# Order of a list-scheduled graph kernel: hand-written ranks or a table of ranks

## Chip, core and metric

One core of a Trainium2 chip runs the whole kernel. The metric is the device time in microseconds (us): the median of three executions, 4420.69 us for the kernel before (4419.77 to 4421.27). The profile is one more execution of the same program; its span, from the first to the last instruction, is 4417.6 us.

## What is computed

Sixteen graphs (B = 16) of 1024 nodes with 256 features pass through four layers. In front of each layer stands a normalisation over the features and a ReLU, and each layer's result is added to x. All graphs share one adjacency matrix.

```python
# layers 0, 1 (one head) and 3 (four heads of 64): graph attention
h = x @ W
e = leaky_relu(e_src[:, :, None] + e_dst[:, None, :])
attention = softmax(where(adj, e, -big), axis=-1)
out = relu(attention @ h)          # layer 0;  elu in layers 1 and 3
# layer 2: eight heads of 32, masked dot-product attention, then
x = layernorm(x + t); h = relu(x @ w1 + b1); x = layernorm(x + h @ w2 + b2)
# around every layer
h = maximum(layernorm(x), 0.0);  x = x + layer(h)
```

## The kernel before

The kernel is written as *operations*. An operation is a small bundle of instructions of one engine with a guessed duration (`cost`), the operations it comes after, the buffers it takes and gives back, and a `rank`. When all are laid, `play()` walks them through a model of the five engines (PE, DVE, ACT, POOL and SP, the queue that issues transfers) and sends out the instructions in the order in which the model began them. Every engine of the chip then runs its instructions in that order and waits at semaphores. All this happens on the host while the program is built. What it decides is the order alone.

```python
DELAY = (0.2, 0.12, 0.14, 0.06, 2.0)
SWITCH = {None: 0.2, 132: 0.21, 32: 0.125}   # PE: change of the form of matmuls
SLACK = 0.1
STAY = 4.0
PLAYS = 8

def choose(open_ops, time, begin, key, slack):
    best = None
    for eng in range(5):
        could = [...]                        # (earliest start, op) of what can begin
        if could:
            last = min(c[0] for c in could) + slack
            at, o = min((c for c in could if c[0] <= last), key=lambda c: key(c[1]))
            ...
def forward(rank):
    ...
    at, o = choose(open_ops, time, begin,
                   lambda o: rank[o.number] + STAY * (o.eng == PE and o.form != form), SLACK)
    ...
def play():
    rank, best = [o.rank for o in ops], None
    for _ in range(PLAYS):
        result = forward(rank)
        if best is None or result[0] < best[0]:
            best = result
        rank = backward(*result)             # latest starts become the next ranks
    ...                                      # then o.fn() in the order of the best play
```

PE's operations have three forms: full (128 x 128 array, `form=None`), 132 (layer 2's scores, 32 rows) and 32 (products with 32 columns). The stages of the graphs are interleaved; between the beginning and the end the order repeats with a period of one graph:

```python
for b in range(1, B - 3):
    order += [(2, b), (1, b + 1), (3, b), (0, b + 2)]     # (layer, graph)
```

A tile of 128 rows that leaves a layer enters the next one at once. This is the end of layer 1 and the way into layer 2, with the durations that the model takes; `TH` = 4 tiles make one half `n` of a graph:

```python
# gat_out, layer 1
inv = op(DVE, 0.08, ...)                     # 1 / sum
o   = op(ACT, 0.73, ...)                     # exp and relu of the product
add = op(DVE, 0.98, ...)                     # two additions into x
way_in(s.next, t, rank, [add])
# way_in, layer 2, for each tile
m_op (DVE 0.54) -> r_op (POOL 1.15) -> norm (ACT 0.4)
# when the four tiles of the half are there
transpose_rows(...)                          # PE 0.88 (tp), ACT 0.92 (hT)
two_values(s, n, ...)                        # PE 3.48, then ACT 0.92
queries_keys(s, m, n, ...)                   # m = 0, 1: PE 3.43 each, then ACT 0.92
```

A stage of layer 3 begins with its sources: `tpr` turns them on PE, DVE copies them, a transfer stores them (`kept`) and two transfers spread them over the partitions (`r`). DVE then makes the weights `p` from `r`, and PE multiplies them (`acc` L1091, `sums` L1115).

Of the kernel before, what the change touches and what calls it, by code (L numbers as in the profile page):

```python
# [28 lines left out]
U8 = mybir.dt.uint8  # L29
I32 = mybir.dt.int32  # L30
AF = mybir.ActivationFunctionType
ALU = mybir.AluOpType
AX = mybir.AxisListType
PSUM = bass.MemoryType.PSUM

P = 128
# [3 lines left out]
H2 = 8  # L40

GAT_HIGH, GAT_LOW = 2.0**45, 2.0**-45
INV_HIGH, INV_LOW = 2.0**80, 2.0**-90


def rows(w):
# [239 lines left out]
def fast_path(tc, bad, x, adj, l0_w, l0_a, l1_w, l1_a, w_qkv, ln1_g, ln1_b, ln2_g, ln2_b, w1, b1, w2, b2, l3_w, l3_a, out):  # L286

    nc = tc.nc
    B, N, C = x.shape
    assert B > 6  # L290
    NT, KC, HALF = N // P, C // P, 512
    NH, TH = N // HALF, HALF // P
    D2 = C // H2
    SCALE2 = 1.0 / float(D2) ** 0.5
    H3, _, HS3 = l3_w.shape
# [4 lines left out]
    with ctx:  # L300
# [9 lines left out]
        xs = {}  # L310
# [99 lines left out]
        WX = {0: wx0, 1: wx1, 2: qkv_sb[:, :, 2 * C :], 3: wx3}  # L410
# [15 lines left out]

        ops = []
        PE, DVE, ACT, POOL, SP = range(5)  # L430

# [5 lines left out]

        BEFORE_END = 0.1

        SLACK = 0.1  # L440

        STAY = 4.0
        PLAYS = 8

        class Op:
# [35 lines left out]
# [4 lines that stand above are left out]
                could = []  # L485
                for o in open_ops[eng]:
                    at = begin(o)
                    if at is not None:
                        could.append((max(at, time[eng]), o))
                if could:  # L490
                    last = min(c[0] for c in could) + slack
                    at, o = min((c for c in could if c[0] <= last), key=lambda c: key(c[1]))
                    if best is None or at < best[0]:
                        best = (at, o)
            assert best, "nothing can begin"
            open_ops[best[1].eng].remove(best[1])
            return best

        def forward(rank):

            time, form, held = [0.0] * 5, 0, {DVE: 0.0, POOL: 0.0}
            ready = [0.0] * len(ops)
            missing = [len(o.after) for o in ops]
            taken = {
                ring: [[h for h in ring.first if h.place == i] for i in range(ring.bufs)] if ring.is_set else [list(ring.first)]
                for ring in R.values()
            }
            left, free = {}, {}
            for ring in R.values():
                for h in ring.first:  # L510
                    left[h], free[h] = len(h.enders), 0.0
            open_ops = [[o for o in ops if o.eng == eng and not o.after] for eng in range(5)]
            played = []

            def places_of(ring):

                times = []
                for i, holds in enumerate(taken[ring]):
                    if not holds or not left[holds[-1]]:
                        times.append((free[holds[-1]] if holds else 0.0, i))  # L520
                return sorted(times)

            def begin(o):
                at = ready[o.number]
                if o.eng == POOL or o.tiles:
                    at = max(at, held[POOL + DVE - o.eng])
                for i, h in enumerate(o.takes):
                    ring = h.ring
                    again = sum(g.ring is ring for g in o.takes[:i])
                    if ring.is_set:  # L530
                        times = places_of(ring)
                        if again >= len(times):
                            return None
                        at = max(at, times[again][0])
                        continue
                    k = len(taken[ring][0]) + again
                    if ring.ordered and h.number != k:
                        return None
                    if k >= ring.bufs:
                        old = taken[ring][0][k - ring.bufs]  # L540
                        if left[old]:
                            return None
                        at = max(at, free[old])
                return at

            for _ in ops:
                at, o = choose(open_ops, time, begin, lambda o: rank[o.number] + STAY * (o.eng == PE and o.form != form), SLACK)
                cost = o.cost
                if o.eng == PE and o.form != form:
                    cost, form = cost + SWITCH[o.form], o.form  # L550
                if o.tiles:
                    held[o.eng] = at + cost - BEFORE_END
                time[o.eng] = at + cost
                played.append((at, cost, o))
                end = at + cost + o.delay
                for h in o.takes:
                    place = places_of(h.ring)[0][1] if h.ring.is_set else 0
                    taken[h.ring][place].append(h)
                    left[h], free[h] = len(h.enders), 0.0
                for h in o.ends:  # L560
                    left[h] -= 1
                    free[h] = max(free[h], end)
                for u in o.users:
                    missing[u.number] -= 1
                    ready[u.number] = max(ready[u.number], end if u.eng != o.eng else end - ITSELF)
                    if not missing[u.number]:
                        open_ops[u.eng].append(u)
            return max(time), played, taken

        def backward(total, played, taken):  # L570

            before = [list(o.after) for o in ops]
            for ring, places in taken.items():
                for holds in places:
                    for old, h in zip(holds, holds[1 if ring.is_set else ring.bufs :]):
                        before[h.taker.number] += [o for o in old.enders if o is not h.taker]
            waiting = [0] * len(ops)
            for list_of in before:
                for o in list_of:
                    waiting[o.number] += 1  # L580
            length, key = [0.0] * len(ops), [0.0] * len(ops)
            for at, cost, o in played:
                length[o.number], key[o.number] = cost, -(at + cost)
            time, ready, latest = [0.0] * 5, [0.0] * len(ops), [0.0] * len(ops)
            open_ops = [[o for o in ops if o.eng == eng and not waiting[o.number]] for eng in range(5)]
            for _ in ops:
                at, o = choose(open_ops, time, lambda o: ready[o.number], lambda o: key[o.number], 0.0)
                time[o.eng] = at + length[o.number]
                latest[o.number] = total - time[o.eng]
                for a in before[o.number]:  # L590
                    waiting[a.number] -= 1
                    ready[a.number] = max(ready[a.number], time[o.eng] + a.delay)
                    if not waiting[a.number]:
                        open_ops[a.eng].append(a)
            return latest

        def play():
            rank, best = [o.rank for o in ops], None
            for _ in range(PLAYS):
                result = forward(rank)  # L600
                if best is None or result[0] < best[0]:
                    best = result
                rank = backward(*result)
            for ring, places in best[2].items():
                for i, holds in enumerate(places):
                    for h in holds:
                        h.place = i
            for _, _, o in best[1]:
                for h in o.takes:
                    h.t = h.make(h.place) if h.ring.is_set else h.make()  # L610
                o.fn()
            return best
# [27 lines left out]
        class Stage:  # L640
# [33 lines left out]
            @property  # L674
            def v(self):
                used = NT * self.heads * (self.hs + 1)
                return self.vh.t[:, :used].rearrange("p (t h d) -> p t h d", t=NT, h=self.heads)

            @property
            def e(self):  # L680
                return self.eh.t

            @property
            def y(self):
                return self.yh.t
# [727 lines left out]
        E = B - 1  # L1413
# [100 lines left out]
        at = 0.0  # L1514
        for k, s in enumerate(stages):
            begin = at
# [11 lines left out]
            if k + 1 < len(stages) and stages[k + 1].layer == 0:  # L1528

                nxt = stages[k + 1]  # L1530
                for t in range(NT):
                    here = x_in[nxt.b]
                    way_in(nxt, t, begin + 1.0 + 3.0 * t, [here[t * len(here) // NT]] + (s.mains[t * len(s.mains) // 12 :][:1] or stages[k - 1].mains[-1:]))
        play()


# [55 lines left out]
```

## Time and profile before

| | |
|---|---|
| median time | 4420.69 us |
| span of the profile | 4417.6 us |
| PE busy | 4314.3 us |
| DVE busy | 3376.2 us |
| ACT busy | 2002.7 us |
| POOL busy | 1274.0 us |
| matmul instructions | 28105 |

The page gives busy time and instructions of each engine, and the chain of work that ended last with shares by engine and by line. The timeline gives instructions in order of time: start, duration of the merged group, engine, line, tiles written and read, count, and in brackets the idle time of the engine before it with what ended it. The end of a matmul is modelled; the distance from one start to the next is the safer length. PEclk is the clock granted to TensorE, 1.00 being full.

### The profile page before, as it was taken

The page shows a single profiled execution, that of the slowest core. Times are in us where ns is not written, and L with a number is a line of the kernel's source. Part 1 is how long each engine was busy: PE and PEld are TensorE (multiplying, and loading weights), DVE is VectorE, ACT ScalarE, POOL GpSimd, SP SyncE. Part 2 cuts the span into 40 slices and gives each one's busy share as a digit, 9 for nine tenths or more (in the row PEclk, how much of TensorE's full clock was granted, in tenths as well). Part 3 has the DMA queues.
Part 4 walks back from the last instruction along what each step waited for, and adds up shares of the span by engine and source line. Part 5 has one row for each costly group of instructions (what it writes and reads, how often), then busy time and mean ns, then how long its engine had stood idle before and what let it go on. Part 6 is the DMA issues. An engine that isn't in the chain of part 4 may idle for free.

```text
span 4417.6 us, 70358 instructions
## 1 busy us (share of the span) xinstructions
PE 4314.3 (98%) x28105; PEld 2232.0 (51%) x28105; DVE 3376.2 (76%) x5834; ACT 2002.7 (45%) x3091; POOL 1274.0 (29%) x2025
## 2 busy tenths in 40 slices
PE   9999999999999999999999999999999999999998
PEld 7735364553545535455354554545545455464433
DVE  7577977778777787777877778777787777858798
ACT  4452635435354353543535435353453534545351
POOL 3222231422324223242222423224232242323121
PEclk9999999999999999999999999999999999999999
DMA  3000000010000000000000000000000000000001
GB/s 109 6 6 25 20 20 30 13 32 6 20 30 20 25 6 25 25 20 25 6 25 25 20 25 6 25 25 20 30 1 25 25 20 30 1 30 1 30 1 40
DMA packets 59598, 96.07 MB, mean 22 GB/s; under 512 B 6280, under 2 KB 41472, under 8 KB 59264
## 3 DMA queue, kind: packets, MB, share of 16 engines
q1 hardware_dynamic: 58848, 90.98, 6.3%
q8 instruction: 223, 3.65, 0.3%
q14 instruction: 111, 0.91, 0.1%
q10 hardware_dynamic: 416, 0.52, 0.0%
HBM read 74.32 MB, written 17.17 MB: 21 GB/s over the span
## 4 chain that ended last, share of the span: by engine, by line
PE 92%; DVE 5%; ACT 2%; POOL 1%; issue 1%; DMA 0%; DVEq 0%; SPq 0%; ACTq 0%; POOLq 0%
PE pm L726 21%; PE av L1001 20%; PE sc L1211 12%; PE acc L1245 11%; PE acc L1091 10%; PE sums L1250 9%; PE sums L1115 5%; PE tp L719 3%; DVE pe L1233 2%; PE tpv L1154 1%; PE tpo L1276 1%; DVE st L695 1%; ACT pe L1225 0%; DVE y L710 0%; ACT hT L722 0%
## 5 line engine op out<-in xcount | busy, mean ns | idle before, releaser
L1233 DVE TENSOR_TENSOR pe<-pe,mask_pos 128x1024 f32<-128x1024 f32 x1024 | 1224.2, 1239 | 203.8 <-ACT pe L1225 202.0
L1225 ACT ACTIVATE pe<-sc 128x1024 f32<-128x1024 f32 x1024 | 992.5, 1022 | 536.5 <-PE sc L1211 515.8
L1001 PE MATMUL av<-v,p 128*128 128x257 f32 x4096 | 941.7, 381 | 1.0 <-ACT o L1023 0.8
L1001 PEld LDWEIGHTS av<-v,p 128*128 128x128 f32 x4096 | 763.7, 190 | 155.4 <-issue 35.6
L1057 DVE SCALAR_TENSOR_TENSOR p<-r,e,mask_pos 128x1024 f32<-128x1024 f32 x512 | 623.3, 1278 | 134.0 <-PE sums L1115 103.0
L699 POOL TENSOR_SCALAR rstd<-stats 128x1 f32<-128x1 f32 x768 | 324.0, 422 | 1258.7 <-DVE stats L696 1235.3
L1211 PE MATMUL sc<-qT,kT 32*128 32x512 f32 x4096 | 601.0, 639 | 6.0 <-ACT pe L1225 5.8
L700 POOL TENSOR_TENSOR rstd<-rstd,minus_half 128x1 f32<-128x1 f32 x768 | 574.9, 749 | 64.0
L1245 PE MATMUL acc<-pe,v 128*32 128x512 f32 x4096 | 563.4, 604 | 0.3
L1250 PE MATMUL sums<-pe,pick 128*32 128x512 f32 x4096 | 550.8, 592 | 0.0
L1091 PE MATMUL acc<-p,v 128*32 128x512 f32 x4096 | 469.8, 593 | 3.0 <-DVE p L1057 3.0
L726 PE MATMUL pm<-l_wx,hT 128*128 128x259 f32 (+1 forms) x1536 | 372.6, 391 | 5.3 <-ACT hT L722 5.2
L1211 PEld LDWEIGHTS sc<-qT,kT 32*128 32x128 f32 x4096 | 167.7, 183 | 398.4 <-ACT pe L1225 254.2
L1310 POOL TENSOR_TENSOR y<-y,turned 128x512 f32<-128x512 f32 x64 | 90.5, 1435 | 923.4 <-DVE turned L1303 923.3
L726 PEld LDWEIGHTS pm<-l_wx,hT 128*128 128x128 f32 x1536 | 287.2, 191 | 96.8 <-issue 33.2
L1250 PEld LDWEIGHTS sums<-pe,pick 128*32 128x32 f32 x4096 | 138.6, 110 | 303.8 <-issue 300.7
L1091 PEld LDWEIGHTS acc<-p,v 128*32 128x32 f32 x4096 | 129.8, 110 | 299.2 <-issue 281.8
L695 DVE BATCH_NORM_STATS2 st<-x 128x6 f32<-128x256 f32 x512 | 213.0, 416 | 78.3 <-POOL x L1027 71.3
L1245 PEld LDWEIGHTS acc<-pe,v 128*32 128x32 f32 x4096 | 88.7, 108 | 344.9 <-DVE pe L1233 152.6
L1027 POOL TENSOR_TENSOR x<-x,o 128x256 f32<-128x256 f32 x128 | 112.3, 877 | 489.1 <-ACT o L1023 487.5
L772 ACT ACTIVATE xn<-x,stats 128x256 f32<-128x256 f32 x256 | 127.7, 508 | 270.1 <-DVE stats L696 248.9
L1115 PE MATMUL sums<-p,e 128*32 128x512 f32 x2048 | 249.4, 593 | 0.0
(104 smaller groups left out, 4207.0 us busy)
## 6 DMA issues: line engine op xcount, KB each, us to landing
r<-kept SPq DMA_DIRECT2D x64, 512.0 KB
x<-in_x_dram SPq DMA_DIRECT2D x32, 512.0 KB
out_dram<-x SPq DMA_DIRECT2D x64, 256.0 KB
r<-kept SPq DMA_DIRECT2D x62, 256.0 KB
edges<-in_adj_dram SPq DMA_DIRECT2D x8, 512.0 KB
kept<-rows_sb SPq DMA_DIRECT2D x128, 2.0 KB
qkv_sb<-in_L_gnn_w_qkv_dram SPq DMA_DIRECT2D x1, 768.0 KB
rows_in<-in_L_gnn_a_dram SPq DMA_DIRECT2D x2, 256.0 KB
```

What stands on the lines that cost most here:

```text
L699: nc.gpsimd.tensor_scalar(rh.t, mh.t[:, 1:2], EPS, None, ALU.add)
L700: nc.gpsimd.tensor_tensor(rh.t, rh.t, minus_half, ALU.pow)
L726: nc.tensor.matmul(dst, lhsT=lhsT[:, k, :], rhs=rhs[:, k, :], start=(k == 0), stop=(k == KC - 1))
L1001: nc.tensor.matmul(avh.t[:, : s.hs + 1], lhsT=phs[part].t[:, j % each, i * P : (i + 1) * P], rhs=s.v[:, j, h, :], start=(j == 0), stop=(j ...
L1057: nc.vector.scalar_tensor_tensor(ph.t[:, hh, :], s.rh[hp].t[:, hh, :], s.e[:, j, col : col + 1], mask_pos[:, j, :], ALU.max, ALU.mult)
L1091: nc.tensor.matmul(acc[n].t[(2 * hh + part) * W : (2 * hh + part + 1) * W, :], lhsT=s.v[:, jj, h, part * W : (part + 1) * W], rhs=p, start ...
L1115: both(lambda jj, n, hh, h, p: nc.tensor.matmul(sums.t[(2 * n + hh) * W : (2 * n + hh + 1) * W, 0, :], lhsT=s.e[:, jj, 2 * H + h : 2 * H + ...
L1211: nc.tensor.matmul(scs[pair].t[:, hh, :], lhsT=s.kh.t[r0 : r0 + D2, g, j * P : (j + 1) * P], rhs=s.qh.t[r0 : r0 + D2, g, cols], start=True ...
L1225: lambda pair=pair: nc.scalar.activation(part(pair), scs[pair].t, AF.Exp, scale=SCALE2),
L1233: lambda pair=pair: nc.vector.tensor_tensor(part(pair), part(pair), mask(), ALU.mult), [ex], tiles=True,
L1245: nc.tensor.matmul(head(acc, i), lhsT=s.v[:, j, g * QUAD + i, :D2], rhs=p(i), start=(j == 0), stop=(j == NT - 1))
L1250: nc.tensor.matmul(head(sums, i), lhsT=pick[:, g, :], rhs=p(i), start=(g == 0 and j == 0), stop=(g == KC - 1 and j == NT - 1),)
```

## The change

The ranks of all operations stand in a table in the program. It was found by a random search over plays of the same engine model. Three printable characters make one rank in base 90; there are 302 lines with 33,435 characters. `play()` takes one forward play with these ranks where the table has three characters for each operation that was laid, and else does the eight plays as before. `STAY`, which added 4.0 to the rank of a PE operation of another form than the last, is gone, and `SLACK` is 0.5 in place of 0.1. Operations, their costs, buffers and the order of the stages are untouched.

```diff
+DIGITS = "#$%&'()*+,-./0123456789:;<=>?@ABCDEFGHIJKLMNOPQRSTUVWXYZ[]^_`abcdefghijklmnopqrstuvwxyz{|}"
+RANKS = (
+    "#&P#%+#&C#(I####%@#$p##d#$Y#%L#$g#%]#%q#&B#&3#&]#%M#'S#&`#'%#'Z#'q#&]#&T#%0#'[#'T#'>#(&#'j#(>#)W#)?#);#(X#)d#*$"
     ... (302 such lines)
+)
-        SLACK = 0.1
-
-        STAY = 4.0
+        SLACK = 0.5
         PLAYS = 8
-                    at, o = min((c for c in could if c[0] <= last), key=lambda c: key(c[1]))
+                    at, o = min((c for c in could if c[0] <= last), key=lambda c: key[c[1].number])
-                at, o = choose(open_ops, time, begin, lambda o: rank[o.number] + STAY * (o.eng == PE and o.form != form), SLACK)
+                at, o = choose(open_ops, time, begin, rank, SLACK)
         def play():
-            rank, best = [o.rank for o in ops], None
-            for _ in range(PLAYS):
-                ...
+            if len(RANKS) == 3 * len(ops):
+
+                digits = [DIGITS.index(c) for c in RANKS]
+                best = forward([(x * 90 + y) * 90 + z for x, y, z in zip(digits[::3], digits[1::3], digits[2::3])])
+            else:
+                rank, best = [o.rank for o in ops], None
+                for _ in range(PLAYS):
+                    ...
```

Read as an order only, the table puts PE's operations where layer 1 of graph 6 ends and layer 3 of graph 5 begins like this (lowest rank first):

```
two_values   layer 2, graph 6, first half
turn
values       layer 1, graph 6   (three of them)
turn
product      layer 3, graph 5   (the last of its projections)
values       layer 1, graph 6   (three, the last ones)
turn
tpr          layer 3, graph 5
queries_keys layer 2, graph 6, m = 0, first half
queries_keys layer 2, graph 6, m = 1, first half
values       layer 3, graph 5   (two of them)
totals       layer 3, graph 5
queries_keys layer 2, graph 6, m = 1, second half
...
two_values   layer 2, graph 6, second half
...
queries_keys layer 2, graph 6, m = 0, second half
```

The places of the table repeat every 155 PE operations from graph to graph there, for graphs 3 to 13.

## The prediction

> **What bounds the kernel now.** I read the page first for the engine with no room, then the chain for what ends the span, then the timeline of one graph's period for where that engine stands still.
>
> ```profile
> span 4417.6 us, 70358 instructions
> ...
> PE 4314.3 (98%) x28105; PEld 2232.0 (51%) x28105; DVE 3376.2 (76%) x5834; ACT 2002.7 (45%) x3091; POOL 1274.0 (29%) x2025
> ...
> PE 92%; DVE 5%; ACT 2%; POOL 1%; issue 1%; DMA 0%; DVEq 0%; SPq 0%; ACTq 0%; POOLq 0%
> ```
>
> PE is busy for 98% and is 92% of the chain that ended last. DVE, the next, has a quarter of the span free. The change adds and removes no instruction, so PE's own work stays; an order can win only what PE loses around it. 4417.6 less 4314.3 leaves 103 us of plain idle time, to which come matmuls that ran slower than they can.
>
> The timeline of PE shows that the loss isn't spread. A graph's period is 273 us (the place shown below comes back every 273 us), and PE runs without a hole in it but for one place, where layer 1 ends:
>
> ```profile
> 1677.85 3.61 PE L726 MATMUL pm<-qkv_sb,hT 128*128 128x256 f32 x16
> 1681.30 3.60 PE L726 MATMUL pm<-hT,qkv_sb 128*128 128x512 f32 x8
> ...
> 1689.09 3.60 PE L726 MATMUL pm<-hT,qkv_sb 128*128 128x512 f32 x8
> ...
> 1697.88 0.27 PE L915 MATMUL tpr<-ident,e 128*96 128x128 f32 x1
> 1697.98 3.65 PE L1001 MATMUL av<-v,p 128*128 128x257 f32 x16
> 1701.47 0.60 PE L719 MATMUL tp<-ident,y 128*128 128x128 f32 x4
> 1703.31 0.44 PE L719 MATMUL tp<-ident,y 128*128 128x128 f32 x2 [1.24 <-ACT y L752]
> 1706.09 0.44 PE L719 MATMUL tp<-ident,y 128*128 128x128 f32 x2 [2.33 <-ACT y L752]
> 1707.64 5.19 PE L726 MATMUL pm<-qkv_sb,hT 128*128 128x256 f32 x16 [1.11 <-ACT hT L722]
> 1712.66 3.60 PE L726 MATMUL pm<-hT,qkv_sb 128*128 128x512 f32 x8
> ```
>
> The reader is to see three idle stretches, 1.24, 2.33 and 1.11 us, in one row: PE has issued the last `av` of layer 1, and all that stands next in its queue needs that product's way through DVE, ACT and POOL. The chain of waits in this window runs inv 1701.67, ex 1701.93, two additions, statistics, POOL's root 1704.16 to 1705.41, y 1705.43, tp 1706.09, hT 1706.56, pm 1707.64: some 6.0 us from the end of `av` (1701.64). The other half's three projections (1677.85, 1681.30, 1689.09), which could have stood here, were already spent before.
>
> **The cost of one seam.** From 1701.47 to 1707.64 are 6.17 us for a transpose bundle that takes 0.88 elsewhere (1675.23 to 1676.11): 5.29 lost. Then `two_values` takes 1707.64 to 1712.66 = 5.02 us, where the same bundle took 1677.85 to 1681.30 = 3.45: 1.57 lost. Together 6.86 us. The same two differences at the eleven other places where `tp<-ident,y` waited 2.33 to 2.34 us (604, 878, 1151, 1426, 1976, ... 3615 us) are 7.5 to 8.1; the twelve sum up to **92 us**, 2.1% of the time. Plain idle time is 56 us of it: tp waited 42.9 us for y in 24 waits, two for each seam, and the projections 13.4 us for hT.
>
> [...] in the 8 us from 1706 the granted clock was 0.79, in the 8 us from 1982, after the next seam, 0.68, against 1.00 from 1714 on. [...] So a seam that is filled gives back its slow matmuls too. [...] what ends each gap is y or hT, the product of a chain of short instructions, and no buffer comes free at that moment. That is a matter of order, which the change can reach.
>
> **The change part by part.**
>
> *The table is used.* 33,435 characters are 11,145 ranks. The operations that are laid come to the same number: layer 2's stages lay 285 each beyond the way in (192 for 32 items, 21 for the outputs, 72 for the feed-forward), 16 x 285 = 4560; layer 3's 1197; layers 0 and 1 1792; the ways in 1536 for statistics and norms, 256 for turns, 192 and 1216 for projections; sources and their limits 80 + 239; start-up 77. The sum is 11,145. So the eight plays are not taken, and the hand-written ranks no longer matter.
>
> *The instructions* stay: the same 28105 matmuls, the same transfers. Reading the table costs the chip nothing, since it is read when the program is built.
>
> *The order at the seam* is what I credit. Sorted by the table's numbers, layer 1's last three `values` are followed by a turn, `tpr` and then two `queries_keys` of the **first** half (m = 0 and m = 1), with `two_values` of the second half and the other two `queries_keys` further down; so for graphs 3 to 13. In the kernel before these two stood at 1681.30 and 1689.09. They need only the first half's hT, so they can run at once: 2 x 3.43 = 6.9 us of work against a hole of 6.0 us. The hole closes, if they are played there. The 6.9 us that they leave behind earlier close up, since PE was saturated there.
>
> Does layer 3 then start too late? In the kernel before `tpr` ran at 1697.88 and DVE began the weights at 1706.15, 8.3 us later; four of some 1.21 us are needed for the first `acc`, so about 13.1 us from `tpr`. In the table `tpr` stands behind the last `av`, some 3.5 us later than before, so `acc` can begin up to 13 us after the last `av`. PE has 2 x 3.43 + 0.88 + 3.48 + 2 x 3.43 = 18.1 us to do until then. It fits.
>
> Eleven graphs follow this pattern; I count the twelfth seam too, since the end is laid differently but has other work. Ranks are wishes and not the played order, and a fresh order brings small waits of its own. I credit three quarters to four fifths of 92: **70 us**.
>
> *The form changes.* I count 1298 of them on PE in the trace. Going from scores to another form costs 0.21 us (eight score matmuls take 1.07 us from start to start, eight of the same width within a run of L1091 0.86), into scores from a product with 32 columns 0.11, between full and 32 some 0.12 to 0.15; in sum about 199 us. Each of the 512 score bundles needs a change in and a change out, 512 x 0.33 = 167 us, so at most some 30 are to be had. Without `STAY` they could as well grow: in the table's sorted order of a period there are 33 changes between full and 32, in the trace's 20. If it were played so, 13 x 0.13 x 13 periods = 22 us would be lost. The model charges for changes, and its charges (0.2, 0.21, 0.125) are near the measured ones, so the search had reason to avoid them. I put 0, give or take 15. [...]
>
> *The end.* From 4300 to 4418 us PE is busy for 97.9 of 118 us, and 6.8 of the rest are the wait for the closing check, which no rank moves. The table orders the last two graphs differently. I credit 5 us.
>
> Sum: 4420.7 - 70 - 0 - 5 = **about 4346 us**.
>
> **Rivals.** (a) *The hole moves.* If two fewer projections ahead of the seam leave PE waiting there for `av` weights from DVE, the gain is lost: for it speaks that DVE has a chain at the same time; against it, that DVE is at 209 of 273 us and PE shows no gap in the 260 us before. It would make 4390 to 4415. (b) *The model's gain isn't the chip's.* An order that is searched for one set of guessed durations may lean on them within tenths of a us; y takes ACT 0.60 us here, the model says 0.4. Each engine works its queue in order, so one late bundle holds the rest. With 155 PE bundles in a period, 0.05 us each would be 100 us over 13 periods and eat the gain. Against it: the old order leaned on the same numbers and left under 4 us a period outside the seam. It would make 4400 or more. (c) *The search finds more than the seam*: all 92 us, 10 to 20 of form changes, 10 at the ends. That makes 4300 to 4320, over 2%.
>
> **Range and chances.** 2% is 88 us, nearly the whole of the seams; it takes rival (c), to which I give 3 in 10. Slower by 2% has no mechanism in view. The range runs from (c)'s middle to the middle of (a).
>
> **What would show it.** Right: PE's plain idle time falls from 103 to about 45 us, tp's waits for y fall from 42.9 to under 10, a graph's period from 273 to about 267 us, and two projections of the other half stand behind the last `av` of layer 1. The seam's granted clock stays at 1.00. DVE's and ACT's busy time stay within 1%. Wrong: the gaps stand as before, or as long ones for `p` at L1001 or L1091; or PE's busy time grows at L1211 and L1250, which would be more form changes. The prediction fails high if rivals (a) or (b) hold, and low if the search also emptied the other 100 us that are lost between the seams and at the ends.

## The result and the profile after

The changed kernel takes **4307.44 us** (median of four, 4306.5 to 4307.8) against 4420.67 us: 0.9744 of the time, 95% interval 0.9727 to 0.9761, 113 us less. The prediction said 4346 us, with a range of 4308 to 4400, about the middle of rival (c) to the middle of (a). It forecast too little: 75 us in place of 113, and the result lies 0.6 us below the lowest edge.

Span, busy time and chain of the page after:

```profile
span 4305.8 us, 70159 instructions
...
PE 4246.3 (99%) x28105; PEld 2207.6 (51%) x28105; DVE 3382.3 (79%) x5834; ACT 2006.0 (47%) x3091; POOL 1239.9 (29%) x2025
...
PE 92%; DVE 4%; ACT 1%; POOL 1%; issue 0%; DMA 0%; SPq 0%; DVEq 0%; ACTq 0%; POOLq 0%
```

The same 28105 matmuls are there, and PE still bounds. Its plain idle time fell from 103 to 60 us (4305.8 less 4246.3), and its busy time by 68 us. The second number is worth a thought: a shorter busy time for the same matmuls means that waits and slow matmuls had been counted as work.

The timeline of PE at the seam, after; lines have moved down by 311 (L1001 is L1312, L726 L1037, L719 L1030):

```profile
1657.16 3.77 PE L1037 MATMUL pm<-l_wx,hT 128*128 128x268 f32 x16
1660.77 1.90 PE L1312 MATMUL av<-v,p 128*128 128x257 f32 x8
1662.51 0.27 PE L1226 MATMUL tpr<-ident,e 128*96 128x128 f32 x1
1662.62 7.03 PE L1037 MATMUL pm<-hT,qkv_sb 128*128 128x512 f32 x16
1669.49 1.04 PE L1030 MATMUL tp<-ident,y 128*128 128x128 f32 x8
1671.68 3.70 PE L1037 MATMUL pm<-hT,qkv_sb 128*128 128x512 f32 x8 [1.15 <-ACT hT L1033]
1675.22 3.62 PE L1037 MATMUL pm<-qkv_sb,hT 128*128 128x256 f32 x16
```

Between the last `av` and the turn stand sixteen matmuls of 512 columns: the two query/key products of the first half, 6.87 us from start to start. y is ready before PE asks for it, so the eight transposes run in one piece. The waits of the turns for y over the whole kernel (us in total, times, longest), before and after:

```profile
PE tp L719 <- ACT y L752: 42.9, 24, 2.3
```

```profile
PE tp L1030 <- ACT y L1063: 0.3, 1, 0.3
```

What is left is 1.15 us for hT. The first product behind the turn takes 3.54 us here, 0.11 more than elsewhere; in the kernel before it lost 1.57. The granted clock fits that: 0.79 over 8 us would be some 1.7 us lost, by estimate (8 x 0.21), and after the change it is 1.00. The windows of 8 us behind the seam, first of before, then of after; the column in front of the last two is PEclk:

```profile
1706.00:1714.00 8.00, 6.80 (x22) 5.05 (x23) 7.85 (x7) 2.07 (x3) 0.00 (x0) 0.79 0.41 160
```

```profile
1671.00:1679.00 8.00, 7.32 (x25) 4.86 (x26) 7.99 (x7) 1.77 (x3) 0.00 (x0) 1.00 0.38 148
```

A graph's period, from one turn of layer 3's sources to the next, fell from 273.1-275.6 us to 265.0-266.0 where the orders repeat.

To see where all of the 113 us came from I took the starts of PE's matmuls in each trace, group by group, and subtracted what a matmul of that shape takes in an undisturbed run (0.107 us for 512 columns in the packed forms, 0.2175 for `av`, 0.429 and 0.216 for the projections, 0.109 for a transpose; 3995 us in all, the same for every kernel here). Of the rest I booked the changes of form at their measured lengths, and what is over 0.3 us by the place where it stands. A *score bundle* is one operation of form 132, eight matmul instructions. The columns and the 3995 us leave about 26 us of each span, its start and its close among them, which stand in no column:

| kernel | time, us | at a turn and the projection behind it | two score bundles in a row (count) | changes of form | other |
|---|---|---|---|---|---|
| before | 4420.67 | 104 | 22.1 (16) | 199 | 71 |
| after | 4307.44 | 21 | 2.8 (2) | 194 | 66 |
| seam_moved | 4354.08 | 35 | 22.1 (16) | 199 | 72 |
| seam_undone | 4379.93 | 97 | 2.8 (2) | 194 | 63 |
| end_after | 4395.78 | 94 | 22.1 (16) | 197 | 61 |
| seam_and_end | 4333.37 | 29 | 22.1 (16) | 197 | 62 |
| dve_block | 4324.73 | 22 | 12.4 (9) | 193 | 75 |
| no_table | 4446.41 | 114 | 6.9 (5) | 209 | 94 |
| ranks_shaken | 4403.17 | 40 | 14.9 (7) | 194 | 133 |
| searched_on | 4285.88 | 6 | 0 (0) | 194 | 62 |

So 83 us came from turns (nearly all at the twelve seams and two turns near the end), 19 from score bundles in a row, 5 from changes of form, 5 from the rest. The second of these has no term in the prediction's sum.

### The profile page after: what moved, and what is told of

The parts are those of the page before. It is cut to its first block, busy times and chain, and to the rows that moved or that the text cites. A ratio compares the mean times of both kernels' runs of the same rounds, so it can differ in the third digit from the quotient of the medians.

```text
span 4305.8 us, 70159 instructions
## 1 busy us (share of the span) xinstructions
PE 4246.3 (99%) x28105; PEld 2207.6 (51%) x28105; DVE 3382.3 (79%) x5834; ACT 2006.0 (47%) x3091; POOL 1239.9 (29%) x2025
## 4 chain that ended last, share of the span: by engine, by line
PE 92%; DVE 4%; ACT 1%; POOL 1%; issue 0%; DMA 0%; SPq 0%; DVEq 0%; ACTq 0%; POOLq 0%
PE pm L1037 21%; PE av L1312 21%; PE sc L1522 12%; PE acc L1556 10%; PE acc L1402 10%; PE sums L1561 9%; PE sums L1426 5%; PE tp L1030 3%; DVE pe L1544 2%; PE tpo L1587 1%; PE tpv L1465 1%; POOL v L1211 1%; DVE st L1006 0%; PE tps L1451 0%; PE tps L1587 0%
## 5 line engine op out<-in xcount | busy, mean ns | idle before, releaser
L1312 PE MATMUL av<-v,p 128*128 128x257 f32 x4096 | 939.9, 381 | 2.9 <-ACT o L1334 2.2
L1312 PEld LDWEIGHTS av<-v,p 128*128 128x128 f32 x4096 | 762.7, 190 | 150.5 <-issue 29.3
L1010 POOL TENSOR_SCALAR rstd<-stats 128x1 f32<-128x1 f32 x768 | 292.2, 381 | 1154.6 <-DVE stats L1007 1115.4
L1522 PE MATMUL sc<-qT,kT 32*128 32x512 f32 x4096 | 588.8, 639 | 1.1 <-ACT pe L1536 1.1
L1011 POOL TENSOR_TENSOR rstd<-rstd,minus_half 128x1 f32<-128x1 f32 x768 | 549.4, 715 | 63.9
L1556 PE MATMUL acc<-pe,v 128*32 128x512 f32 x4096 | 552.6, 603 | 0.2
L1561 PE MATMUL sums<-pe,pick 128*32 128x512 f32 x4096 | 540.9, 592 | 0.0
L1037 PE MATMUL pm<-l_wx,hT 128*128 128x259 f32 (+1 forms) x1536 | 367.2, 387 | 2.8 <-ACT hT L1033 2.0
L1037 PEld LDWEIGHTS pm<-l_wx,hT 128*128 128x128 f32 x1536 | 286.9, 190 | 62.4 <-issue 14.3
L1556 PEld LDWEIGHTS acc<-pe,v 128*32 128x32 f32 x4096 | 87.8, 108 | 350.4 <-issue 149.1
L1037 PE MATMUL pm<-hT,qkv_sb 128*128 128x512 f32 x512 | 229.8, 595 | 14.1 <-ACT hT L1033 14.1
```

The costliest lines, as they stand in the source:

```text
L1010: nc.gpsimd.tensor_scalar(rh.t, mh.t[:, 1:2], EPS, None, ALU.add)
L1011: nc.gpsimd.tensor_tensor(rh.t, rh.t, minus_half, ALU.pow)
L1037: nc.tensor.matmul(dst, lhsT=lhsT[:, k, :], rhs=rhs[:, k, :], start=(k == 0), stop=(k == KC - 1))
L1312: nc.tensor.matmul(avh.t[:, : s.hs + 1], lhsT=phs[part].t[:, j % each, i * P : (i + 1) * P], rhs=s.v[:, j, h, :], start=(j == 0), stop=(j ...
L1522: nc.tensor.matmul(scs[pair].t[:, hh, :], lhsT=s.kh.t[r0 : r0 + D2, g, j * P : (j + 1) * P], rhs=s.qh.t[r0 : r0 + D2, g, cols], start=True ...
L1556: nc.tensor.matmul(head(acc, i), lhsT=s.v[:, j, g * QUAD + i, :D2], rhs=p(i), start=(j == 0), stop=(j == NT - 1))
```

## The experiments

A play of ranks that simply number a kernel's own played order gives that order again. So each experiment but the one of the constants is a table of its own in the changed program, and its edit is one of the order; the diffs below write it as assignments to ranks. PE's order in the traces of the first two differs from that of the kernel they start from at the seams alone. Times are medians; single executions of one kernel differ by up to 6 us (4350.9 to 4356.8 in the first experiment). The kernel before measured 4422.87 us beside the two seam experiments, the end and the constants, and 4421.19 us beside the other four.

**The seam alone, in the old order.**

```diff
 # old order; for graphs b = 3 .. 13, layer 2
+rank[queries_keys(b, m=0, n=0)] = rank[last values of layer 1, graph b] + 0.1
+rank[queries_keys(b, m=1, n=0)] = rank[last values of layer 1, graph b] + 0.2
```

> The kernel before, its played order written down as a table (which alone gives the same order), with one edit: for graphs 3 to 13 the two query/key products of the first half stand behind the last product of layer 1. Theory S, the seam: each of the eleven seams loses 6.9 to 8.1 us before and some 1.3 us after, so about 11 x 6.3 = 69 us fall away: 4350 us, between 4340 and 4365. Rival D, the gain is spread over the whole order, and moving two products alone only moves the hole ahead of the seam: 4395 us or more.

4354.08 us, 0.9848 of the kernel before (0.9831 to 0.9864): 68.8 us less. Theory S holds. Two bundles out of some 155 of a period carry three fifths of the whole gain. By the account above nothing else changed: 104 fell to 35 us in the column of turns, the others stayed within 1 us. PE at graph 6's seam of this kernel:

```profile
1675.48 7.03 PE L1037 MATMUL pm<-hT,qkv_sb 128*128 128x512 f32 x16
1682.35 1.04 PE L1030 MATMUL tp<-ident,y 128*128 128x128 f32 x8
1684.54 3.72 PE L1037 MATMUL pm<-qkv_sb,hT 128*128 128x256 f32 x16 [1.15 <-ACT hT L1033]
```

It is the same picture as in the changed kernel, and no new hole opened in front of it.

**The seam undone, in the new order.**

```diff
 # new order; for graphs b = 3 .. 13
+rank[queries_keys(b, m=0, n=0)] = rank[two_values(b, n=0)] + 0.1
+rank[queries_keys(b, m=1, n=0)] = rank[last values but one] - 0.1
+rank[tpr of layer 3, graph b-1]  = rank[last values] - 0.1
```

> The changed kernel's played order as a table, with one edit: for graphs 3 to 13 the two query/key products of the first half go back to where the kernel before had them, one behind two_values, one ahead of the last products of layer 1, and tpr ahead of the last one. Theory S: the holes of 4.7 us and their slow matmuls come back, 4307 + 69 = 4376 us, between 4362 and 4385. Rival D: at most 4330 us, since all else stays.

4379.93 us: 72.5 us more than the changed kernel, or 70 when each is set against the runs of the kernel before beside it. The seam is worth nearly the same from both sides. In eight of the eleven graphs the two products are all that moved in PE's order; `tpr`, whose rank was put ahead of the last `values` too, got there in three graphs only. At graph 6 the wait is in one piece:

```profile
1687.55 0.82 PE L1030 MATMUL tp<-ident,y 128*128 128x128 f32 x6
1692.06 0.69 PE L1030 MATMUL tp<-ident,y 128*128 128x128 f32 x2 [3.69 <-ACT y L1063]
1693.86 6.09 PE L1037 MATMUL pm<-hT,qkv_sb 128*128 128x512 f32 x8 [1.11 <-ACT hT L1033]
1699.80 3.62 PE L1037 MATMUL pm<-qkv_sb,hT 128*128 128x256 f32 x16
```

The projection behind it takes 5.94 us to the next start in place of 3.43. In the window of 8 us that holds it the granted clock is 0.58:

```profile
1692.00:1700.00 8.00, 6.83 (x11) 3.05 (x12) 2.50 (x3) 1.03 (x3) 0.00 (x0) 0.58 0.77 262
```

**The end alone.**

```diff
 # old order up to tpr of layer 3, graph 12; behind it the new order
+rank = old position if new start <= new start of tpr(3, 12) else 10**7 + new position
```

> The kernel before's order until layer 3 of graph 12 turns its sources (3612 us in its trace), the changed kernel's order behind that. Reading of the two traces: loss beyond matmuls and changes of form behind that point is 40.3 + 7.9 us before and 16.8 + 8.4 after, so 23 us: 4420.7 - 23 = 4398 us, between 4390 and 4404. The prediction had credited 5 us: 4416 us. Rival D, a gain that needs the whole order: 4415 or more.

4395.78 us: 27.1 us less, not the 5 that the prediction gave to the end. It contains the seam of graph 13, which lost 7.5 us before and 1.3 after, so some 21 us belong to the last three graphs proper. There the old order had two more turns with holes (at 4300 and 4325 us, 4.0 and 3.7 us lost ahead of a projection and 4.5 behind). Of these 12 us some 3.4 remain. The table puts another 10 us under "other" (71 to 61), which were not taken apart.

**Both together.**

> Both earlier edits of the old order at once: the two products moved at graphs 3 to 13, and the changed kernel's order behind the turn of layer 3's sources of graph 12 (where the seam of graph 13 falls in the new part). They measured -68.8 and -27.1 us alone, each against the same runs of the kernel before. Theory S, separate stretches of PE's queue that add up, less the one seam of 6 to 8 us that both contain: 4423 - 89 = 4334 us, between 4326 and 4340; some 27 us of the change then lie elsewhere, in the periods. Rival D, they lean on each other: under 4315 or over 4345.

4333.37 us, 87.8 us less than the kernel before: the parts add up, and 26 us of the change are still missing. The table says where: 19 us at score bundles in a row (22.1 against 2.8), and 8 us at turns (29 against 21). Some 5 of the 8 lie at the seam of graph 2, which neither edit touched; it lost 6.8 us here and 2.1 in the changed kernel.

**DVE's ranks alone.** In the kernel before, PE takes two score bundles in a row at sixteen places. One stood out in the timeline of PE and DVE, before, once the starts are compared:

```profile
2147.90 1.04 PE L1250 MATMUL sums<-pe,pick 128*32 128x512 f32 x8
...
2148.88 1.99 PE L1211 MATMUL sc<-qT,kT 32*128 32x512 f32 x12
...
2150.05 3.77 ACT L1225 ACTIVATE pe<-sc 128x1024 f32<-128x1024 f32 x4 [0.99 <-PE sc L1211]
...
2151.13 1.13 PE L1211 MATMUL sc<-qT,kT 32*128 32x512 f32 x4 [0.27 <-ACT pe L1225]
2151.50 0.48 DVE L710 SCALAR_TENSOR_TENSOR y<-y,rstd,be_sb 128x256 f32<-128x256 f32 x1
...
2152.89 1.22 DVE L1233 TENSOR_TENSOR pe<-pe,mask_pos 128x1024 f32<-128x1024 f32 x1
```

Twelve score matmuls in a group of 1.99 us, then four more at 2151.13: the second half of the second bundle waits for ACT to read a pair of banks of the first. The program has three such pairs, and a bundle takes two. The hole is 1.38 us by the starts, of which the trace shows 0.27 as idle. DVE stood in a row of statistics and norms until 2152.89, so no masked product was ready for PE. The two bundles in a row are not a choice made on the chip, though: the play laid them, in the model. The edit puts such rows of DVE back and leaves PE's ranks alone:

```diff
 # new order; at 15 places of layer 2
+for op in statistics, norms, additions that the old order had ahead of the masks:
+    rank[op] = rank[first mask of that item] - 0.5   # in one block, old order
```

> The changed kernel's played order, with an edit on DVE alone: at fifteen places of layer 2, where the kernel before laid two score bundles of PE in a row, the statistics, norms and additions that it had run on DVE just ahead of the masks are put there again in one block. PE's own ranks stay. Theory P: the masks come late, PE finds no product ready, takes two score bundles in a row in about nine of the places and stands some 1.4 us at each, with about 0.6 us behind: 4307 + 9 x 2.0 = 4325 us, between 4315 and 4335. Rival: DVE has over 20% of the span free, its order inside a stretch is hidden, 4303 to 4311 us.

4324.73 us: 17.3 us more than the changed kernel. Seven new places appear (nine with the two that stayed), each with the 1.38 us:

```profile
2105.18 1.99 PE L1522 MATMUL sc<-qT,kT 32*128 32x512 f32 x12
2107.43 1.13 PE L1522 MATMUL sc<-qT,kT 32*128 32x512 f32 x4 [0.27 <-ACT pe L1536]
2108.49 1.09 PE L1030 MATMUL tp<-ident,y 128*128 128x128 f32 x8
```

They make 9.6 us, and some 9 more stand under "other". The waits of scores for ACT in the view of this tile (us, times) go the same way as the count of places, 16, 2 and 9; before, after and this kernel:

```profile
  ACT pe L1225: 5.8, 19
```

```profile
  ACT pe L1536: 1.1, 3
```

```profile
  ACT pe L1536: 2.9, 10
```

So the rival, that DVE's ranks don't matter since DVE has a fifth of the span free, falls. But PE's order did not stay: with DVE's work late in the model, the play laid PE's bundles in another order too, in seven graphs, and the seven new places stand there. How much the late masks cost with PE's order held was not run. Nor does the 17 us measure the 19 of the table: only 9.6 us of it are score bundles in a row, and this is the reverse of the change at a part of its places, not its undoing.

**The constants alone.**

```diff
-RANKS = ( ... )
+RANKS = ""
```

> The changed kernel with an empty table: eight plays from the hand-written ranks, SLACK 0.5, no STAY. Theory T, the table carries the gain and the two constants only suit it: 4420 to 4450 us, no gain. Rival K, dropping STAY and widening SLACK give a good part by themselves: under 4400 us.

4446.41 us, 1.0053 of the kernel before: dropping `STAY` and widening `SLACK` win nothing by themselves and cost 24 us. Changes of form grow by 10 us, the small waits by 23, while score bundles in a row fall to five. Without the table there is no gain; the table with the old constants was not run.

**The ranks shaken.**

```diff
+rank += gauss(0, 0.5 us), each operation by itself
```

> The changed kernel's table with a random number added to each of the 11,145 ranks by itself, of mean 0 and standard deviation 5 (the ranks' unit is a tenth of a us, so 0.5 us). Theory F: the ranks are a tuned seed of one play, and what they win hangs on single choices of one out of several that could begin within SLACK: the gain is lost, over 4400 us, with score bundles in a row and holes at the seams again. Rival R: the broad order is what counts: under 4330 us.

4403.17 us: 95.7 of the 113 us are gone after a shake of half a us. Theory F holds in its time, and in part in its signs: score bundles in a row come back (14.9 us), but the seams stay mostly closed (40 us at turns against 21). Most of the loss is in small waits, which double, 66 to 133. This is one draw of random numbers, and whether the play in the model grew as much is not on record.

**A further search.**

```diff
-RANKS = ( ... )
+RANKS = ( ... )   # found from these ranks; same random number for the same operation of all graphs
```

> The changed kernel with another table, found by searching on from its ranks over plays of the same engine model, where one random number is added to the same operation of all graphs at once. At the seam it lays one query/key product, two_values of the first half, the turn, and only then the other query/key product of the first half, so that PE has 3.4 us of work while ACT turns out hT. Theory S: the hT wait of 1.15 us and the start behind it, 1.3 us in each of twelve seams, go: 4307 - 16 = 4291 us, and up to 6 less if the two remaining score pairs and small waits go too: 4283 to 4293. Rival M: further gains of the model are within its error by now, 4300 to 4312 us.

**4285.88 us**, 0.9694 of the kernel before (0.9681 to 0.9708), 21.6 us below the changed kernel. It is the version that beats both. Its seam:

```profile
1649.58 3.60 PE L1037 MATMUL pm<-hT,qkv_sb 128*128 128x512 f32 x8
1653.01 0.27 PE L1226 MATMUL tpr<-ident,e 128*96 128x128 f32 x1
1653.12 3.62 PE L1037 MATMUL pm<-qkv_sb,hT 128*128 128x256 f32 x16
1656.58 1.04 PE L1030 MATMUL tp<-ident,y 128*128 128x128 f32 x8
1657.45 3.60 PE L1037 MATMUL pm<-hT,qkv_sb 128*128 128x512 f32 x8
1660.89 3.62 PE L1037 MATMUL pm<-qkv_sb,hT 128*128 128x256 f32 x16
```

One product of the first half was kept back until behind the turn, and PE works while ACT turns out hT. So it is at eleven of the twelve seams; that of graph 2 keeps its 1.15 us. The column of turns falls from 21 to 6 us, no score bundles stand in a row, and the rest is 4 us smaller. Those three make 22 us, as measured.

## Why the prediction was wrong

- **The mechanism at the seam was right.** The chain of 6 us, the two products as its filling, layer 3 in time behind them, and the clock came as written. y made tp wait 42.9 us before and 0.3 after, and the granted clock behind the seam of graph 6 is 1.00 in place of 0.79. The credit of 70 us for twelve seams came close to the 74 measured (by the starts, 92 us lost before and 18 after), but partly by luck: it held back a fifth to a quarter for ranks that aren't played and for new small waits. The small waits fell, and what stayed is the wait for hT, which the prediction took as closed.
- **"It runs without a hole in it but for one place" was the step that failed.** The other holes of a period hid in groups that look busy: twelve score matmuls in 1.99 us, and a wait of 1.38 us of which 0.27 was booked as idle. I read idle times in brackets and busy totals, not starts. Rows of DVE work ahead of the masks, and the score bundles taken in a row because of them, were no term of the sum. Such bundles lost 22.1 us before and 2.8 after, so 19 us were missing there.
- **"The end" was mis-sized:** 5 us credited, 27 measured, 21 without the seam in it, so 16 us were missing here. These two steps make 35 of the 39 us between 4346 and 4307. I set PE's busy share of the last 118 us against the closing check and left out the 700 us ahead, where the order differs too.
- **Changes of form** at 0 give or take 15 were right: 5 us fewer. The table's sorted order, with its 33 changes between full and 32, is not the played one.
- **Rivals.** (a), the hole moves, is refuted by the seam moved alone. (b), the model's gain isn't the chip's, fell too in what it foretold: each of the two orders that the search preferred was faster on the chip, by 113 and by a further 21.6 us, and no new row of small waits ate it (71 us before, 66 and 62 after). What the model itself promised is not on record. (c) came in total, 4307 inside its 4300 to 4320, but by other terms: 74 us of the 92, 5 from changes of form in place of 10 to 20, 21 at the end in place of 10, and 19 from score bundles, which it did not name.
- **The range** ended at the middle of (c), to which I had given 3 in 10; it cut half of that rival off, and the result lies 0.6 us in the part cut off.
- **"Plain idle time falls to about 45 us"** was 60, mainly because at each seam 1.15 us for hT stayed, 14 us over twelve.

What a change of form costs is measured; its cause stays open. Within one form, in the trace of before, weight loads of the full array run beside matmuls of the full array, sixteen of which take 3.49 us from the first start to the next operation's (1697.98 to 1701.47), 0.218 us each:

```profile
1697.88 3.35 PEld L1001 LDWEIGHTS av<-v,p 128*128 128x128 f32 x16
1697.98 3.65 PE L1001 MATMUL av<-v,p 128*128 128x257 f32 x16
```

What the gaps of PE left of the granted clock is measured at four seams. In the 8 us behind, a gap of 3.69 us and one of 1.11 left a clock of 0.58; 1.24, 2.33 and 1.11 us in a row 0.79 and 0.68; 1.15 us alone 1.00. By what rule the clock falls is not shown.

The seams needed no more buffers: moving two products was enough. At the score bundles in a row the wait is one for a bank; still, with the same banks the new order has two such places in place of sixteen. More banks were not tried.

## What to carry to other kernels

Where one engine is busy for 98%, look for the few places where all that its queue holds next hangs on the chain behind its last product, and keep independent work of that length back for them: two bundles kept back won 69 us of 4421. Compare starts, not busy time: of a wait of 1.38 us inside a group the trace showed 0.27 as idle. And the ranks of an engine with a fifth of its span free can still cost the bound one time: 17 us here, about half of it through the order that the play then gave to PE.

## What the runs showed that I had not expected

An order that is found by search over a simple engine model was faster on the chip, and a second step of the search won a further 21.6 us. Yet its ranks are brittle, in the one draw that was run: a shake of its ranks by 0.5 us, far under the length of most bundles (0.88 to 3.48 us on PE), cost 95.7 us. The two edits of the played order, in contrast, add up to within 2 us: 68.8 and 27.1 alone, less the 6 us of the seam in both, and 87.8 together.
